# A two-layer decoder on one core: two contexts' values computed earlier and kept in memory, and a new order of the work behind the experts

## The chip, the cores and the metric

The kernel runs on one core of a Trainium2 chip. The time is device microseconds (us) of the whole program on that core; lower is better. TensorE is called PE (its weight loads PEld), VectorE DVE, ScalarE ACT, GpSimd POOL and SyncE SP.

## What is computed

Four sequences (B = 4) of 512 tokens with 256 features pass through six sublayers, each followed by a layer norm: a test-time-training layer, a softmax attention with an additive table (`fside`) over a context of 1601 rows, a mixture of eight experts (two per token), a causal self attention with 16 heads of 16, a 16-head cross attention over the same context with rotated queries and keys, and a feed-forward layer. Everything is float32. The part that the change is about is the cross attention, cut to what matters:

```python
K = (ctx @ Wk.T + bk) -> 16 heads, rotated       # ctx: (4, 1601, 256)
V = (ctx @ Wv.T + bv) -> 16 heads
x = layernorm(x + (softmax(Q K^T / 4 + mask) V) @ Wo.T + bo)
```

The values V need nothing but the context and one 256 x 256 weight (`xaV`; the bias goes into `bob`), so they can be computed at any time.

## The kernel before, in words

**Stages.** The program is one long body, in which each engine's order is mostly written out by hand (`tc.manual_schedule()`); what stands between two such regions is placed by a planner among the neighbours on the same engine. Memory on the core is taken in pools that are closed and opened like a stack, so tiles of a later pool lie where those of a closed one were.

*Test-time training* (ttt, to about 242 us), then *attention with `fside`* (to about 487 us). There `steps` runs over 4 sequences x 4 blocks of 128 tokens: `scored` (L654), `turned` (L684), `weighted` (L706), three blocks deep. The transposed context `ctxT` of a sequence is loaded whole (L639); those of sequences 2 and 3 are in memory when the loop ends. When a sequence's four blocks are done, its `closing` (L719) follows in pieces, one per call of `tail()`: moments and root, the normalization, the transposition `to_xT`, then `route` (L462: the router's matmul on PE, softmax and two choices on DVE, a matmul for the places, then the rows on DVE). For sequences 0 to 2 the next blocks' work fills PE in between; for sequence 3 nothing is left. Behind it stand `scatter(B - 1)` (L772: eight indirect DMAs on POOL that put token rows in `xs`) and `blocks_left` (L773, one small matmul and some 25 small DVE operations), both outside the hand-written order.

*Experts* (L821 on, to about 1024 us): weights for all later stages are loaded first on SP (L824 to L828), then `begin(0)` loads the first rows `xb` from `xs`; 23 blocks of 256 rows follow.

*Behind the experts* (L1588 to L1612): the experts' results are gathered and summed for sequence 0 (`combined(0)`: `fetch`, then `add`, whose last entries are the root and the scaling of the layer norm, then `turn`, the two transpositions), and on PE come the values of contexts 0 and 1 and the keys of context 0 (`keys0`, rotated by DVE at L1149 to L1152), the first self-attention keys and queries (`k0_`, `q0_`) and values (`self_values`, L1134). Each of these takes one of four PSUM banks (`one()`), which ACT empties. Keys go through DRAM (`to_rows`, `from_rows`) to get one head per 32 partitions.

*Attention* (L1638 on): 32 units, 16 of self attention and 16 of cross attention, one for each sequence and group of four heads. A cross unit takes 13 steps of 128 keys. Each step computes scores on PE twice: pass 1 for the next unit (`slot1`, L1229, whose maxima DVE takes at L1267) and pass 2 for this one (`scores`, L1303; exponentials on ACT at L1324), and multiplies the exponentials with the values (`weighted`, L1327). A step has two halves. Other PE work hangs in lists, `extras[i]` for unit i, of which one item goes into a step: with an item, the step's first half carries the whole 512-wide `weighted` and the second half the item; without one, each half carries a 256-wide `weighted` (L1669 to L1684). Among the items are keys (`key`, L1176, rotated on POOL) and values (`value`, L1186: two 256-wide matmuls, each shown as two records, and one ACT copy) of contexts 2 and 3. They are spread by `later` (L1613): 12 key items beside sequence 0's units, 4 key items and 13 values beside sequence 1's, 13 values beside sequence 2's. Their input comes in pieces of 512 columns, two at a time (`chunk`, L1162). The values live in two tiles, `vals[b % 2]`.

Of the kernel before, what the change touches and what calls it, by code (L numbers as in the profile page):

```python
# [9 lines left out]
F32 = mybir.dt.float32  # L10
# [7 lines left out]
P = 128  # L18
B, S, D = 4, 512, 256
S2 = 1601  # L20
NT = S // P
# [13 lines left out]
def kn_of(kt):  # L35
    return P if kt < NKT - 1 else KLAST
# [3 lines left out]
def decoder(ctx: ExitStack, tc: tile.TileContext, a: dict, out: bass.AP):  # L40
# [564 lines left out]
        return wrow, xrow  # L605


    with tc.tile_pool(name="p2", bufs=2) as p2, ExitStack() as ordered:


# [73 lines left out]
        def turned(b, t):  # L684

            sc = scs.pop((b, t))
            pT = p2.tile([P, NKT, P], F32, tag="pT", name="pT")
            for k0 in (0, 8):
                ps = wide()
                flat = ps.rearrange("p a n -> p (a n)")  # L690
                for kt in range(k0, min(k0 + 8, NKT)):
                    kn = kn_of(kt)
                    nc.tensor.transpose(
                        flat[:kn, (kt - k0) * P : (kt - k0 + 1) * P], sc[:, kt * P : kt * P + kn], ident
                    )
# [46 lines left out]
        scored(*steps[0])  # L742
        tails = []

        def tail():
            if tails and next(tails[0], tails) is tails:
                tails.pop(0)

        for i in range(len(steps) + 1):
            if i + 1 < len(steps):  # L750
                b, t = steps[i + 1]
                scored(b, t)
                if t == NT - 1:
                    more_columns(b + 2)
                    if b + 1 < B:
                        queries(b + 1)
            tail()
            if i < len(steps):
                turned(*steps[i])
            tail()  # L760
            if i > 0:
                b, t = steps[i - 1]
                weighted(b, t)
                if t == NT - 1:
                    if b + 1 < B:
                        ctxns[b + 1] = load_ctx(b + 1)
                    tails.append(closing(b))
            tail()
        while tails:
            tail()  # L770
        ordered.close()
        scatter(B - 1, lambda inst: unordered("xs", inst))  # L772
        wrow, xrow = blocks_left()  # L773
    ph2in.close()


# [2 lines left out]


    QS = 1.0 / math.sqrt(HD)
    VW = HD + 1
# [243 lines left out]
    with ExitStack() as s4:  # L1026
# [827 lines left out]
```

## Time and profile before

| | |
|---|---|
| median of three runs | 2437.19 us (2430.2 to 2437.96) |
| the profiled execution, its own time | 2439.88 us |
| its span, first to last instruction | 2438.0 us |
| busy share of the span | PE 96%, DVE 50%, ACT 44%, POOL 17% |

The span by stage, from the trace (the clock is the share of full TensorE speed that was granted):

| us | stage | PE busy | clock |
|---|---|---|---|
| 242 to 487 | attention with `fside` | 240.67 | 0.97 |
| 487 to 523 | `closing(3)`, `blocks_left`, scatter, first `xb` | 10.12 | 0.54 |
| 523 to 1024 | experts | 496.11 | 0.99 |
| 1024 to 1072 | behind the experts | 44.27 | 0.96 |
| 1072 to 1482 | self-attention units | 397.14 | 0.94 |
| 1482 to 1730 | cross units of sequence 0 | 248.00 | 0.98 |
| 1730 to 1976 | of sequence 1 | 246.00 | 1.00 |
| 1976 to 2184 | of sequence 2 | 208.00 | 1.00 |
| 2184 to 2314 | of sequence 3 (no pass 1 for a next unit at its end) | 129.48 | 1.00 |

How to read it: a row of a timeline gives start, duration, engine, line of the kernel, operation, output and inputs, count, and in brackets how long the engine had been idle and what ended that. Matmuls are pipelined, so the durations of neighbours on PE overlap, and the distance between starts says more than the duration. A line such as L202 is that of the helper `mm`, through which most matmuls go; the tile names tell them apart.

### The profile page before, as it was taken

Reading aid. Unit: us, or ns where it says so; the run is one execution under the profiler, and the core shown is the slowest. Engines: PE = TensorE matmul, PEld = TensorE weight load, DVE = VectorE, ACT = ScalarE, POOL = GpSimd, SP = SyncE. Lnnn points to the kernel's source line nnn. Section 1 sums busy time; section 2 is a strip of 40 time slices with the busy share of each in tenths; the row PEclk is TensorE's granted clock in tenths of the full one; section 3 lists DMA queues with packets and bytes.
Section 4 is the critical chain, followed back from the end, with each engine's and each line's share of the span. In section 5 each row is a group of like instructions: output and inputs, shape, how many; then the busy total and the mean of one; then the engine's idle time right before and its main releaser. Section 6 shows DMA issues by size and latency. Waiting matters only on the chain.

```text
span 2438.0 us, 34867 instructions
## 1 busy us (share of the span) xinstructions
PE 2344.4 (96%) x13928; PEld 1328.2 (54%) x13928; DVE 1211.7 (50%) x2854; ACT 1073.5 (44%) x1996; POOL 422.7 (17%) x429
## 2 busy tenths in 40 slices
PE   7898999959999999989999999999999999999998
PEld 4767677748888888843333334333333333333256
DVE  1333334322222233266656667666666666677334
ACT  1111122114444544424555453655666566566730
POOL 1010001121144433345130010222110010000000
PEclk9999999969999999989999997999999999999999
DMA  8300311145667555351211210112110110100100
GB/s 307 150 1 3 124 54 45 49 143 186 247 239 266 198 204 201 124 164 50 66 48 35 95 36 5 39 51 60 51 37 16 45 36 16 30 34 18 31 9 26
DMA packets 76112, 215.84 MB, mean 89 GB/s; under 512 B 11816, under 2 KB 35630, under 8 KB 66862
## 3 DMA queue, kind: packets, MB, share of 16 engines
q1 hardware_dynamic: 61790, 133.04, 16.1%
q0 software_dynamic: 10992, 65.54, 7.3%
q10 hardware_dynamic: 3168, 15.03, 1.8%
q8 instruction: 110, 1.80, 0.3%
q14 instruction: 52, 0.43, 0.1%
HBM read 171.53 MB, written 53.21 MB: 92 GB/s over the span
## 4 chain that ended last, share of the span: by engine, by line
PE 51%; ACT 1%; DVE 1%; issue 0%; DVEq 0%; ACTq 0%
PE s L1310 23%; PE one L202 12%; PE po L1337 11%; PE s L202 2%; PE s L1320 1%; PE one L1295 1%; PE one L1358 1%; ACT x L171 0%; ACT ex L1324 0%; DVE one L1269 0%; PE one L1379 0%; PE one L1477 0%; PE one L1400 0%; DVE pm L1267 0%; DVE st L156 0%
## 5 line engine op out<-in xcount | busy, mean ns | idle before, releaser
L1324 ACT ACTIVATE ex<-s 128x512 f32<-128x512 f32 (+1 forms) x1062 | 577.9, 594 | 466.9 <-PE s L1310 236.7
L1267 DVE TENSOR_REDUCE pm<-one 128x1 f32<-128x512 f32 x768 | 493.7, 685 | 174.5 <-PE s L1310 123.3
L1310 PE MATMUL s<-q,kc 32*128 32x512 f32 x1612 | 524.1, 640 | 0.2 <-ACT ex L1324 0.2
L202 PE MATMUL one<-kc,qt 32*128 32x512 f32 (+1 forms) x2048 | 483.8, 564 | 0.3 <-DVE pm L1267 0.3
L1310 PEld LDWEIGHTS s<-q,kc 32*128 32x128 f32 x1612 | 161.6, 179 | 210.9 <-issue 175.5
L1337 PE MATMUL po<-ex,v 128*32 128x256 f32 (+3 forms) x2472 | 245.1, 465 | 0.3 <-ACT ot L1350 0.3
L1269 DVE CUSTOM_DVE_ANT_0 one<-one,c_diagq 128x512 f32<-128x512 f32 x256 | 171.9, 716 | 75.6 <-PE one L202 63.5
L1310 PE MATMUL s<-q,ks 32*128 32x512 f32 x512 | 179.8, 650 | 5.3 <-ACT ex L1324 4.9
L1337 PEld LDWEIGHTS po<-ex,v 128*32 128x32 f32 (+1 forms) x2472 | 49.8, 108 | 232.2 <-issue 225.5
L886 DVE TENSOR_TENSOR g<-g,sg 128x1024 f32<-128x1024 f32 x46 | 57.2, 1243 | 235.8 <-ACT sg L883 235.7
L202 PE MATMUL wide<-xbT,eWi 128*128 128x256 f32 x736 | 168.9, 389 | 4.0 <-DVE xbT L858 4.0
L202 PEld LDWEIGHTS one<-kc,qt 32*128 32x128 f32 x2048 | 164.2, 188 | 11.6 <-DVE pm L1267 7.9
L202 PE MATMUL wide<-xbT,eWg 128*128 128x256 f32 x736 | 162.6, 379 | 0.0
L202 PE MATMUL bank<-eWo,g 128*128 128x256 f32 x736 | 162.5, 379 | 0.0
L202 PEld LDWEIGHTS wide<-xbT,eWi 128*128 128x128 f32 x736 | 143.5, 196 | 25.8 <-issue 4.2
L202 PE MATMUL one<-ks,qt 32*128 32x512 f32 x512 | 152.6, 665 | 3.7 <-ACT raw L1182 2.7
L202 PEld LDWEIGHTS wide<-xbT,eWg 128*128 128x128 f32 x736 | 139.7, 190 | 19.2 <-ACT g L883 0.2
L1150 POOL TENSOR_TENSOR raw<-raw,c_cos 128x512 f32<-128x512 f32 (+1 forms) x32 | 34.9, 1092 | 660.5 <-DVE swp L1149 578.1
L202 PEld LDWEIGHTS bank<-eWo,g 128*128 128x128 f32 x736 | 138.2, 190 | 17.9
L883 ACT ACTIVATE g<-wide,eWi 128x256 f32<-128x256 f32 x184 | 71.7, 476 | 72.3 <-PE wide L202 69.7
L1310 PEld LDWEIGHTS s<-q,ks 32*128 32x128 f32 x512 | 53.8, 185 | 83.4 <-issue 62.0
L202 PE MATMUL wide<-ctxT,q 128*128 128x512 f32 (+1 forms) x256 | 91.3, 510 | 0.8 <-DVE q L649 0.8
(319 smaller groups left out, 2988.4 us busy)
## 6 DMA issues: line engine op xcount, KB each, us to landing
xs<-zero SPq DMA_DIRECT2D x32, 512.0 KB
kc<-kcd SPq DMA_DIRECT2D x16, 800.5 KB
eWo<-in_eWo SPq DMA_DIRECT2D x8, 1408.0 KB
cx<-in_ctxT SPq DMA_DIRECT2D x18, 512.0 KB
eWi<-in_eWi SPq DMA_DIRECT2D x8, 1028.0 KB
eWg<-in_eWg SPq DMA_DIRECT2D x8, 1028.0 KB
qt<-qd SPq DMA_DIRECT2D x32, 256.0 KB
ctxT<-in_ctxT SPq DMA_DIRECT2D x4, 1601.0 KB
```

The lines of the kernel that those rows point to most:

```text
L202: nc.tensor.matmul(ps, l, r, start=(i == 0), stop=(i == n - 1))
L883: nc.scalar.activation(dst[:, k, :], pv[:, k, :], func, bias=bias)
L886: nc.vector.tensor_tensor(part, part, dst, ALU.mult)
L1150: eng.tensor_tensor(raw[:, :n], raw[:, :n], cos[:, :n], ALU.mult)
L1267: nc.vector.tensor_reduce(pm[:, t, j, c : c + 1], ps, AX.X, ALU.max)
L1269: nc.vector.tensor_tensor_reduce(out=ps, in0=ps, in1=diagq[:, 384 - t * P : 896 - t * P], scale=1.0, scalar=LOWEST, op0=ALU.add, op1=ALU.m ...
L1295: nc.tensor.transpose(pt[:, t * P : (t + 1) * P], ng.rearrange("p j r -> p (j r)"), ident)
L1310: nc.tensor.matmul(ps[:kn], kt[rows, k * P : k * P + kn], q2[rows, :], start=True, stop=cross)
L1320: nc.tensor.matmul(ps[:, k * P : (k + 1) * P], later_[:, :P], later_[:, P:], start=False, stop=True)
L1324: nc.scalar.activation(ex[:kn, h, :], ps[:kn], AF.Exp)
L1337: nc.tensor.matmul(state["po"][j * 32 : j * 32 + 32, q0:q1], (vals if cross else vself)[b % 2][:kn, k, c0 : c0 + 32], ex[:kn, j % 2, q0:q1 ...
L1358: nc.tensor.transpose(pt[:, t * P : (t + 1) * P], ot[:, t * P : (t + 1) * P], ident)
```

## The change

Four things, all in one edit:

1. The 26 values of contexts 2 and 3 (13 blocks of 128 rows each) are computed at the end of the attention with `fside`, from `ctxTs[2]` and `ctxTs[3]`. They stand in three portions in the order of PE and ACT: 3 behind the last `weighted` and the first piece of `closing(3)`, 6 behind the router's matmul and softmax, 17 behind the matmul of `blocks_left`. Two values share a two-bank PSUM tile, a bank each. Their destination is the memory of `fside` (22 blocks) and of half the context rows (4 blocks); `rows_of_values` sets the zeros and ones there on DVE. `blocks_left` moves into the hand-written order, in front of the 17 values, and `scatter(B - 1)` stays behind.
2. Three DMAs on SP write these blocks to two new DRAM tiles `vd` (1.9 MB each): 9 blocks of context 2 behind the ninth value, all 13 of context 3, the last 4 of context 2. The weight `xaV` is loaded once more, early in the stage.
3. In the cross units the 26 values are gone, and with them their eight pieces of context. `later` is now the 8 key items of context 2 beside sequence 0's units and the 8 of context 3 beside sequence 1's. At the start of the second unit of sequences 1 and 2 one DMA on SP reads the next but one values tile from `vd`.
4. Behind the experts `add` stands behind the eighth of context 1's values instead of the thirteenth, `turn` in front of `keys0[4:6]` instead of behind, and `self_values(0)` behind the last keys instead of in front of them.

```diff
+    VW = HD + 1
+    VROW = NH * VW + HD - 1
+    vd = {b: tc.dram_tile((P, NKT * VROW), F32, name=f"vd{b}") for b in (2, 3)}
...
+        xaV = weight(p2, "xaV")
+        values, places, halves = [], {}, []
+
+        def rows_of_values(first):
+            name, tag, n = ("v23", "fs", 22) if first else ("v2", "ctxa", 4)
+            t = p2in.tile([P, NT * S2 if first else KHALF * D], F32, tag=tag, name=name)
...
+            nc.vector.memset(places[3 if first else 2, NKT - 1], 0.0)
+            t = t[:, : n * VROW].rearrange("p (k r) -> p k r", r=VROW)
+            nc.vector.memset(t[:, :, NH * VW :], 0.0)
+            heads = t[:, :, : NH * VW].rearrange("p k (h r) -> p k h r", r=VW)
+            nc.vector.memset(heads[:, :, :, HD : HD + 1], 1.0)
+
+        def value(b, k):
+            kn = kn_of(k)
+            if not halves or len(halves) == 2:
+                halves[:] = [wide()]
+            else:
+                halves.append(halves[0])
+            ps = halves[0][:, len(halves) - 1, :D]
+            mm(ps[:kn], [(ctxTs[b][:, c, k * P : k * P + kn], xaV[:, c, :]) for c in range(2)])
+            dst = places[b, k][:kn, : NH * VW].rearrange("p (h r) -> p h r", r=VW)
+            nc.scalar.copy(dst[:, :, :HD], ps[:kn].rearrange("p (h r) -> p h r", r=HD))
+            if (b, k) == (2, 8):
+                nc.sync.dma_start(vd[2][:, : 9 * VROW], big_of(2, 0, 9))
+            if (b, k) == (3, NKT - 1):
+                nc.sync.dma_start(vd[3], big_of(3, 0, NKT))
+            if (b, k) == (2, NKT - 1):
+                nc.sync.dma_start(vd[2][:, 9 * VROW :], big_of(2, 9, NKT))
...
             if i < len(steps):
                 turned(*steps[i])
+            else:
+                rows_of_values(True)
...
-        while tails:
-            tail()
+        order = [(2, k) for k in range(9)] + [(3, k) for k in range(NKT)]
+        order += [(2, k) for k in range(9, NKT)]
+        values = [lambda b=b, k=k: value(b, k) for b, k in order]
+        for n in (3, 0, 0, 0, 0, 0, 6, 0, 0, 0, 0, 0):
+            if len(values) < len(order):
+                tail()
+            if len(values) == len(order) - 3 and len(places) == 22:
+                rows_of_values(False)
+            for f in values[:n]:
+                f()
+            values = values[n:]
+        assert not tails
+        wrow, xrow = blocks_left()
+        for f in values:
+            f()
         ordered.close()
         scatter(B - 1, lambda inst: unordered("xs", inst))
-        wrow, xrow = blocks_left()
...
-        for f in keys0[0:2] + values1 + add + keys0[4:6] + turn:
+        for f in keys0[0:2] + values1[:8] + add + values1[8:] + turn + keys0[4:6]:
             f()
-        for f in (k0_, q0_, rows0, *self_values(0), *keys0[2:4], *keys0[6:8]):
+        for f in (k0_, q0_, rows0, *keys0[2:4], *keys0[6:8], *self_values(0)):
             f()
...
-        later = [
-            context(2, range(4), ()) + context(3, range(2), ()),
-            context(3, range(2, 4), ()) + context(2, (), range(4)),
-            context(3, (), range(4)),
-        ]
+        later = [context(2, range(4), ()), context(3, range(4), ())]
+        for b in (2, 3):
+            starts[index[b - 1, 1, True]].append(
+                lambda b=b: nc.sync.dma_start(vals[b % 2].rearrange("p k r -> p (k r)"), vd[b])
+            )
```

More of the change, by code (lines that the diff above doesn't have):

```diff
@@ L743, in decoder, with big_of @@
         tails = []
+        xaV = weight(p2, "xaV")
[3 more added lines that the diff above has]
+            t = p2in.tile([P, NT * S2 if first else KHALF * D], F32, tag=tag, name=name)
+            for i in range(n):
+                at = (3, i) if first and i < NKT else (2, i - NKT) if first else (2, 9 + i)
+                places[at] = t[:, i * VROW : (i + 1) * VROW]
+            nc.vector.memset(places[3 if first else 2, NKT - 1], 0.0)
[19 more added lines that the diff above has]
+                nc.sync.dma_start(vd[2][:, 9 * VROW :], big_of(2, 9, NKT))
+        def big_of(b, k0, k1):
+            first = places[b, k0]
+            return bass.AP(first.tensor, first.offset, [first.ap[0], [1, (k1 - k0) * VROW]])
         def tail():
@@ L781, in decoder @@
     QS = 1.0 / math.sqrt(HD)
-    VW = HD + 1
     p4a = late_a.enter_context(tc.tile_pool(name="p4a", bufs=1))
```

## The prediction

> **What bounds the kernel now.** I read the page's busy shares and slices first, then its chain, then the stages, then the timeline at the two places that the change touches.
>
> ```profile
> PE 2344.4 (96%) x13928; PEld 1328.2 (54%) x13928; DVE 1211.7 (50%) x2854; ACT 1073.5 (44%) x1996; POOL 422.7 (17%) x429
> ...
> PE   7898999959999999989999999999999999999998
> ...
> PEclk9999999969999999989999997999999999999999
> ...
> PE 51%; ACT 1%; DVE 1%; issue 0%; DVEq 0%; ACTq 0%
> PE s L1310 23%; PE one L202 12%; PE po L1337 11%; PE s L202 2%; PE s L1320 1%; PE one L1295 1%; PE one L1358 1%; ACT x L171 0%; ACT ex L1324 0%; DVE one L1269 0%; PE one L1379 0%; PE one L1477 0%; PE one L1400 0%; DVE pm L1267 0%; DVE st L156 0%
> ```
>
> PE ends everything that the chain names. One slice, the ninth, is half empty at a low clock: the end of `closing(3)`. In the cross units PE is never free: the list of waits for PE from 1482 to 2314 holds 0.5 us in all. So an item taken from these units shortens the run by its PE time, and one put into the hole costs nothing until the hole is full.
>
> **Part 3, what leaves the cross units.** The groups of lines show the values, and the stage table of this tile that the 104 records of contexts 2 and 3 lie in the units of sequences 1 and 2. The timeline gives one value and the two forms of `weighted`:
>
> ```profile
> 2007.49 1.13 PE L202 MATMUL one<-xaV,cx 128*128 128x256 f32 x4
> ...
> 2060.62 1.06 PE L1337 MATMUL po<-ex,v 128*32 128x512 f32 x8
> ```
> ```profile
> 2064.62 0.64 PE L1337 MATMUL po<-ex,v 128*32 128x256 f32 x8
> ```
>
> By starts: a value holds PE 1.06 us (2007.49 to the scores at 2008.55); the wide `weighted` 0.99 (2060.62 to 2061.61), a half one 0.57 (2064.62 to 2065.19). A step that loses its item goes back to two halves, 1.14 for 0.99. So a value is worth 1.06 - 0.15 = 0.91 us. As a check, the copies of the finished sums (L1350) mark the units' ends: sequence 2's first three take 160.3 us with 10 values and one query item, sequence 3's first three 149.8 with none. Less the query item (2.0 - 0.15), that is 8.7 / 10 = 0.87. I take 0.88: **26 x 0.88 = 22.9 us less**. Ends: the records' whole busy time, 29.3 us; and the worst single pair of units (sequence 2's first 55.3 with 4 values, sequence 3's first 53.6 without), 0.43 each, 11 us. The second would hold if another engine were late next. In a bare half step (1.64 us) ACT is busy 1.08 and DVE 1.29, so both still wait for PE.
>
> Key items only move (12 and 4 become 8 and 8), between units that PE bounds: nothing. Eight pieces of context (SP, 0.46 us an issue) go. The two loads of 1.9 MB stand in SP's queue with key rows, queries and pieces behind them. They overwrite a tile last read by the `weighted` that ended a unit earlier (1706 for a load at 1763), so they don't wait, and DMA is busy 0.10 to 0.15 in these stages. Nothing; if they did hold SP, the rows behind them have a unit's lead.
>
> **Part 1, the hole.** Before, it runs so:
>
> ```profile
> 487.23 0.48 DVE L715 SCALAR_TENSOR_TENSOR r<-bank,rs,x 128x256 f32<-128x256 f32 x1 [4.28 <-PE bank L202]
> ...
> 490.37 2.30 PE L188 MATMUL wide<-ident,x 128*128 128x128 f32 x8 [3.19 <-DVE x L726]
> ...
> 492.71 1.01 ACT L196 COPY xT<-wide 128x1024 f32<-128x1024 f32 x1 [2.84 <-PE wide L188]
> ...
> 505.49 0.64 PE L202 MATMUL bank<-both,before 128*128 128x32 f32 x2 [5.75 <-DVE both L492]
> ```
> ```profile
> 508.35 0.17 DVE L521 SCALAR_TENSOR_TENSOR rows<-eks,ranks 128x8 int32<-128x8 f32 x1 [0.17 <-DVE upto L555]
> ...
> 517.63 0.96 POOL L534 DMA_INDIRECT xs<-x,rows  x1 [0.30 <-issue]
> 520.17 0.89 SPq L835 DMA_DIRECT2D xb<-xs  x2
> ...
> 522.99 1.09 PE L854 MATMUL bank<-ident,xb 128*128 128x128 f32 x4 [15.80 <-DMA xb<-xs]
> ```
>
> The chain is weighted, normalization, router, rows at 508.5, eight scatters at 1.27 us, `xb` issued 520.2, landed 523.0. A value in a row costs 0.89 us at full clock (32 records, 7.14 us at 1024). Portion by portion:
> - 3 values, 2.7 us, fit before the transpositions (487.2 to 490.4). Their copies (0.37 each) stand on ACT behind the root (489.9) and end before the `xT` copy.
> - In two-microsecond windows the clock is 1.00 until 488 and 0.50 from 490 to 530. Now PE works until 489.9, so the transpositions take the 1.04 us that sequence 2's took, and I let the router's matmuls take 3.4 (461.2 to 464.6) for 6.0. The chain gains 1.2 + 2.6 us. [...]
> - 6 values, 5.3 us, lie beside DVE's 5.7 us of choices (499.8 to 505.5); the places' matmul behind them is not held.
> - 17 values are 15.1 us of PE. They begin at 507.2 - 3.8 = 503.4 and end at 518.5, the copy 0.4 later. The scatters now start near 504.8 and have landed near 516.5, so **PE's values take their place as what ends last**: the third store, and with it SP, is free near 519, and `xb` is issued at 519.5 for 520.2.
> - The stores: the zero rows that SP wrote early moved 405 GB/s, so 1.9 MB take 4.7 us. The big one goes out near 515, the last (0.6 MB) at 519; both are through near 522, and `xb` behind them lands near 524.5. That is **1.5 us more** than before. Ends: 1 less (nothing in its way) and 4 more (router cold, stores half as fast).
> - PE is idle some 5 us before `xb`, so the experts' first 32 matmuls stay slow (10.1 us): no gain there.
>
> DVE's new memsets have no row. POOL's of 195 and 208 columns took 0.28 and 0.46, DVE's copy of 512 columns 0.69; three of these are at most 2.1 us in a 4.3 us wait for PE, and three more lie in the 8.5 us behind the normalization: nothing. `blocks_left` no longer interleaves with the rows, which frees 0.2 us of them.
>
> **Part 4, behind the experts.** ACT's root waited for the thirteenth value (row at 1055.24) though DVE was done at 1050.25. Now root and scaling end near 1053.3, but the last five copies stand behind them, and PE has four banks for five values, so it still leaves the values at 1054.9. The transpositions come at 1055.0 instead of 1058.2, but two keys (3.6 us) now stand between them and `k0_`: 1059.6 for 1059.74. Nothing. `self_values` go into the wait for the rows, but need banks that the last two keys hold until ACT reads them (1075.64 and 1077.04, kept by stores of earlier keys). The first scores come near 1077.6 instead of 1072.1; DVE is turning keys until 1078.1 anyway and starts its first maximum near 1079.3 for 1078.2. I take **0.5 us more**; ends -1.5 and +2.
>
> **Sum.** -22.9 + 1.5 + 0.5 = -20.9 us. The profiled execution took 2439.88 (span 2438.0 and 1.9 around it): 2419.0. It stands 2.7 above the median, so 2416 on that scale.
>
> **Rivals**, on the same scale:
> - *The next stage's weight loads go in front of `xb`.* Twelve loads on SP (487.22 to 493.5, 2 MB) lie where the values now lie, and the list of waits shows that the first waited for PE's last `weighted`, the last reader of that memory. Now they wait for the third store, near 522. They stand outside the hand-written order, so the planner may put them before `xb`: 6.2 us of issues, 2 MB in front, `xb` near 531, 8 us late. -22.9 + 8 + 0.5 = -14.4: 2423. For it: they stand first in the text. Against: `xb` is ready a little earlier.
> - *The values were nearly free in the units.* Price 0.43: -11.2 + 2 = -9.2: 2428. For it: that one pair of units; against: all others.
> - *The hole can't take them:* the clock stays at 0.50 there, a value costs 1.7 us (two copies behind the 2.07 us gap at 1048 stand 1.66 apart), 17 take 29, the end is 14 to 18 us later, and the change doesn't do what it says: -22.9 + 18 + 0.5 = -4.4, 2433. Against: PE's gaps are now 0.5 to 1.1 us.
> - *Slower: the stores are slow.* `xb` stands behind them on SP's queue. The key rows (256 KB in rows of 2 KB) took 5.9 us to land, 44 GB/s; at that rate 2.5 MB from 515 on end at 572, and `xb` is 49 us late: +26, 2463. It decides from 23 us late on: 2.5 MB in 30 us, 83 GB/s. Against: the zero rows' 405 GB/s, and 14.9 KB in one piece for each partition.
>
> **Numbers.** Forecast 0.56, weights first 0.22, free values 0.08, hole too small 0.10, slow stores 0.04. A difference of about 0.3% (7.3 us) is the least that a measurement of this kernel can tell from no change: the first three are faster by more, 0.86; the fourth the same, 0.10; the fifth slower, 0.04. The range goes from 2406 (values at 29.3 us, hand-over 1 us shorter) to 2429 (free values); fourth and fifth are left out.
>
> **What would show it.** Right: no L202 on `xaV` from 1482 on; units of sequences 1 and 2 together some 23 us shorter; PE's ninth slice full; the first `xb` matmul within 4 us of 523; the first maximum near 1079. Wrong: the loads of `qkvQ` to `xaO` ahead of `xb`; clock 0.50 during the 17 values; PE waiting for ACT or DVE in bare steps; a wait of SP at the loads from `vd`.

## The result, and the profile after

The changed kernel takes 2431.36 us in the median of 20 runs, the kernel before, on the same chip, 2433.05 us in the median of 20: a ratio of 0.9983, 95% interval 0.997 to 0.9995. That is about 4 us less (1.2 to 7.3; the two medians are 1.7 us apart); 21 us less were forecast. The profiled execution took 2431.25 us, with a span of 2429.5.

The busy shares, the slices and the chain of the changed kernel's page, to be laid beside those of before:

```profile
PE 2343.2 (96%) x14144; PEld 1333.4 (55%) x14144; DVE 1214.0 (50%) x2860; ACT 1075.7 (44%) x1996; POOL 423.6 (17%) x429
...
PE   7898999979999999989999999999999999999998
...
PEclk9999999989999999999999998999999999999999
...
PE 50%; DVE 1%; ACT 1%; issue 0%; DVEq 0%; ACTq 0%
PE s L1368 23%; PE po L1395 12%; PE one L202 11%; PE s L202 2%; PE s L1378 1%; PE one L1353 1%; PE one L1416 1%; ACT x L171 0%; ACT ex L1382 0%; DVE pm L1325 0%; DVE one L1327 0%; PE one L1437 0%; PE one L1535 0%; PE one L1458 0%; DVE nb L166 0%
```

The ninth slice is fuller (7 for 5) and its clock higher (8 for 6): PE does work there now. But PE's busy time is only 1.2 us less, though 26 values moved out of the units: they are the same work in another place, and the gain can only be the time in which PE had been idle. The other weak clock slice, the 25th, lies at the end of the self-attention units, where before has one too (7).

Cut at the same events, the two profiled executions compare like this. "Lost" is the time that PE lost to a half clock, summed over the clock records (length times one minus the granted share); where PE had nothing to do meanwhile, it is more than the clock cost.

| stretch | before (lost) | after (lost) | change | forecast |
|---|---|---|---|---|
| start to the last sum on `r` | 487.23 | 485.00 | -2.2 | 0 |
| the hole: to the first transposition of `xb` | 35.76 (16.6) | 45.98 (4.6) | **+10.2** | +1.5 |
| experts | 501.01 (7.3) | 501.37 (7.3) | +0.4 | 0 |
| hand-over: to the first self-attention maximum | 54.20 (4.1) | 57.01 (3.4) | +2.8 | +0.5 |
| self-attention units | 409.57 (25.6) | 405.22 (20.5) | -4.4 | 0 |
| cross units | 826.09 (1.1) | 810.91 (3.4) | **-15.2** | -22.9 |
| end | 124.15 (3.0) | 123.97 (1.6) | -0.2 | 0 |

The fifth row is clock (409.57 - 25.6 = 384.0, 405.22 - 20.5 = 384.7). The first is not: more was lost to the clock there after (17.1 us) than before (15.4). But this stretch took 482.3 to 487.2 us in the six kernels of this document in which its code is that of before, so its 2.2 us can't be put down to the change. The gain in the units is there, two thirds of its size, and the hole takes two thirds of that back.

The timeline of the changed kernel in the hole (start, duration, engine, line, operation; in brackets the idle time before it and what ended it):

```profile
485.00 0.48 DVE L720 SCALAR_TENSOR_TENSOR r<-bank,rs,x 128x256 f32<-128x256 f32 x1 [3.24 <-PE bank L202]
...
487.55 0.36 ACT L776 COPY v<-wide 128x256 f32<-128x256 f32 x1
...
487.96 1.99 PE L202 MATMUL wide<-xaV,ctxT 128*128 128x256 f32 x8 [2.13 <-ACT v L776]
...
489.79 1.04 PE L188 MATMUL wide<-ident,x 128*128 128x128 f32 x8
...
505.00 0.30 PE L202 MATMUL bank<-both,before 128*128 128x32 f32 x2
...
506.74 0.17 DVE L521 SCALAR_TENSOR_TENSOR rows<-eks,ranks 128x8 int32<-128x8 f32 x1 [0.19 <-DVE eks L516]
...
510.53 1.99 PE L202 MATMUL wide<-xaV,ctxT 128*128 128x256 f32 x8 [0.46 <-ACT v L776]
...
511.70 0.37 ACT L776 COPY v<-wide 128x256 f32<-128x256 f32 x1 [1.22 <-PE wide L202]
...
512.57 0.37 ACT L776 COPY v<-wide 128x256 f32<-128x256 f32 x1 [0.49 <-PE wide L202]
...
512.99 1.99 PE L202 MATMUL wide<-xaV,ctxT 128*128 128x256 f32 x8 [0.46 <-ACT v L776]
...
516.18 0.96 POOL L534 DMA_INDIRECT xs<-x,rows  x1 [0.31 <-issue]
...
526.73 0.32 SPq L782 DMA_DIRECT2D vd<-v  x1
527.14 1.38 SPq L893 DMA_DIRECT2D xb<-xs  x2
...
530.98 1.09 PE L912 MATMUL bank<-ident,xb 128*128 128x128 f32 x4 [4.68 <-DMA xb<-xs]
```

Two things are to be seen. PE is not free to run through the values: eight records (two values) start every 2.46 us, at 510.53 and 512.99, and each time PE has waited 0.46 us for a copy of ACT. And POOL has issued the last scatter by 517.1, but `xb` is issued at 527.1, directly behind the third store, which waited for the last value.

Theory A: two values in one two-bank tile wait for each other. The second value of a pair writes the other bank, but its matmul still waits until ACT has read the first. In the row of 487.96 the second value even waits 2.13 us, since the first one's copy stands on ACT behind the root. Rival: the pace is that of ACT's copies, of the clock or of the matmuls. Theory B, for the units: a bare half step (one without an item) is not bounded by PE alone; rivals are the clock and values that are cheap on PE.

### The profile page after: what moved, and what is told of

It reads as the page before. It is cut to its first block, busy times and chain, and to the rows that moved or that the text cites. A ratio compares the mean times of both kernels' runs of the same rounds, so it can differ in the third digit from the quotient of the medians.

```text
span 2429.5 us, 35297 instructions
## 1 busy us (share of the span) xinstructions
PE 2343.2 (96%) x14144; PEld 1333.4 (55%) x14144; DVE 1214.0 (50%) x2860; ACT 1075.7 (44%) x1996; POOL 423.6 (17%) x429
## 3 DMA queue, kind: packets, MB, share of 16 engines
q1 hardware_dynamic: 60606, 137.66, 16.6%
## 4 chain that ended last, share of the span: by engine, by line
PE 50%; DVE 1%; ACT 1%; issue 0%; DVEq 0%; ACTq 0%
PE s L1368 23%; PE po L1395 12%; PE one L202 11%; PE s L202 2%; PE s L1378 1%; PE one L1353 1%; PE one L1416 1%; ACT x L171 0%; ACT ex L1382 0%; DVE pm L1325 0%; DVE one L1327 0%; PE one L1437 0%; PE one L1535 0%; PE one L1458 0%; DVE nb L166 0%
## 5 line engine op out<-in xcount | busy, mean ns | idle before, releaser
L1368 PE MATMUL s<-q,kc 32*128 32x512 f32 x1612 | 529.5, 640 | 0.8 <-ACT ex L1382 0.8
L1395 PE MATMUL po<-ex,v 128*32 128x256 f32 (+3 forms) x2688 | 252.2, 444 | 0.3 <-ACT ot L1408 0.3
```

Of the source, the lines that this page charges most:

```text
L1368: nc.tensor.matmul(ps[:kn], kt[rows, k * P : k * P + kn], q2[rows, :], start=True, stop=cross)
L1395: nc.tensor.matmul(state["po"][j * 32 : j * 32 + 32, q0:q1], (vals if cross else vself)[b % 2][:kn, k, c0 : c0 + 32], ex[:kn, j % 2, q0:q1 ...
```

## The experiments: the hole

**Own tiles.** Each value takes a new tile and leaves its second bank unused.

```diff
-            if not halves or len(halves) == 2:
-                halves[:] = [wide()]
-            else:
-                halves.append(halves[0])
-            ps = halves[0][:, len(halves) - 1, :D]
+            ps = wide()[:, 0, :D]
```

> The changed kernel, but every value gets a two-bank PSUM tile of its own (one bank used), instead of sharing one with the next value. Measured so far: from the last sum of the attention with the table (DVE's row on r) to the first transposition of xb the kernel before took 35.8 us, the changed one 46.0. Theory A (two values in one tile: the second waits for ACT's copy of the first, so a pair takes 2.46 us): the 17 values then follow each other at 0.89 us, 15.1 instead of 20.7 us, the six earlier ones end about 2 us earlier, and the stretch takes 38 to 40 us; the whole run is 6 to 8 us shorter than the changed kernel, near 2424 where before has 2433. Rival (the pace is set by ACT's copies, by PE's clock or by the matmuls themselves): a pair still takes about 2.4 us and the stretch stays at 45 to 47 us.

Measured: ratio to before 0.9952 (0.9939 to 0.9964), 11.7 us less; the hole is 41.1 us. Its timeline:

```profile
505.89 14.92 PE L202 MATMUL wide<-xaV,ctxT 128*128 128x256 f32 x68
...
521.24 0.32 SPq L778 DMA_DIRECT2D vd<-v  x1
524.09 0.91 SPq L889 DMA_DIRECT2D xb<-xs  x2
...
527.10 1.08 PE L908 MATMUL bank<-ident,xb 128*128 128x128 f32 x4 [6.29 <-DMA xb<-xs]
```

The 17 values (68 records) take 14.9 us in one run without a gap: theory A holds, and the forecast's 15.1 was right for values that don't share a tile. The hole is 1 us longer than expected, though, since `xb` now goes out 2.9 us behind the last store. SP's list of waits names the reason:

```profile
SPq L889 <- DMA xs<-x,rows: 2.5, 1, 2.5
```

The last scatter was issued at 517.75 and the 1.9 MB store at 517.8; from 518 to 524 the DMA engines moved 358 to 424 GB/s (windows of 2 us). Scatters and store collide now.

**Smaller stores, on SP and on ACT's queue.** Both build on own tiles.

```diff
-            if (b, k) == (2, 8):
-                nc.sync.dma_start(vd[2][:, : 9 * VROW], big_of(2, 0, 9))
...
+            for c, k0, k1 in ((2, 0, 3), (2, 3, 9), (3, 0, 4), (3, 4, 8), (3, 8, NKT), (2, 9, NKT)):
+                if (b, k) == (c, k1 - 1):
+                    nc.sync.dma_start(vd[c][:, k0 * VROW : k1 * VROW], big_of(c, k0, k1))
```

> Values in tiles of their own, as in e1_own_tiles (17 values in 14.9 us, but xb issued at 524.1, 2.9 us behind the third store, since the last scatters landed late; hole 41.1 us), and the values go out in six stores instead of three (3, 6, 4, 4, 5, 4 blocks), each when its last block is copied. Theory C (the 1.9 MB store issued at 517.8 fills the DMA engines just when the last scatters and xb want them): the last big piece is 0.7 MB, the scatters land near 519 to 520, xb goes out right behind the last store at 521.3 to 521.7, hole 38 to 39 us. Rival (the scatters are late for another reason, such as POOL's order): xb stays 2.5 to 3 us behind the last store, hole near 41.

> As e5_six_stores, but the stores are issued from ACT's queue instead of SP's, so that xb on SP doesn't stand behind them. Theory C with SP's order as the next limit: xb is issued when the scatters have landed, near 519.5 to 520.5, hole 37 to 38 us. Rival 1 (the values on PE or the weight loads hold xb): as e5, 38 to 39. Rival 2 (issuing on ACT delays the copies and so PE): values at over 0.95 us each, hole over 40.

Measured: six stores on SP 0.9932 (0.9916 to 0.9949), hole 40.0 us; on ACT's queue 0.9918 (0.9888 to 0.9948), hole 40.2. Both missed their 37 to 39. The collision is gone (in the first, `xb` goes out at 521.9 even before the last store), but from the ninth or tenth of the 17 values on ACT's copies come late, several of them 1.41 to 1.46 us apart, and SP's list says that `xb` waits for PE's last matmul on `wide` (1.6 and 2.5 us). So `xb` is tied to the values in a way that I had not counted, and no queue helps it. Presumably its memory is that of something these matmuls read; which tile that is was not followed up.

**One value beside ACT's copy of `xT`.** First alone on the changed kernel, then together with own tiles, stores on ACT's queue and the old order behind the experts:

```diff
-        for n in (3, 0, 0, 0, 0, 0, 6, 0, 0, 0, 0, 0):
+        for n in (3, 0, 0, 0, 1, 0, 5, 0, 0, 0, 0, 0):
```

> The changed kernel with one number list changed: the portions are 3, 1, 5, 17 instead of 3, 6, 17, so that one value lies between the transpositions and the router's matmuls. Pairs of values still share a tile, the stores stay on SP. Theory D (that one value keeps PE's clock at 1.00 through the router's matmuls): rows, 21.7 us behind the last sum in the changed kernel, come 18 to 19 us behind it; the 17 values still take 20.7 us, so xb moves by the same 3 us: hole 42.5 to 43.5 us for 46.0. Rival (only the freed stores and tiles of e7_one_beside_copy made the difference there): hole 45 to 46.

> As e6_stores_on_act, with the old order behind the experts, and the portions 3, 1, 5, 17 instead of 3, 6, 17: one value lies between the transpositions and the router's matmuls, beside ACT's copy of xT. If PE's clock falls at 492 because the window before holds too little work, the added value keeps it up, the router's matmuls take 3.4 to 4 us instead of 5.6, the places' matmul comes 2 to 4 us earlier, and the hole shrinks to 34 to 36 us, less than before. Rival (the clock falls during the router's short matmuls whatever stands before them): the router and the 5 values still run at 0.50, and only one value's time is won, hole 36 to 38. Old order: first values to first maximum 50 to 54 us instead of 56 to 57.

Measured: alone 0.9955 (0.9938 to 0.9971), hole 45.5, so the rival was nearer: three of the four router blocks run at full clock in the changed kernel too, and pairs of values still wait. (The ratio is lower than the changed kernel's 0.9983, with intervals that touch, but the two profiled executions are only 0.6 us apart, so nothing is read from that.) Together 0.9926 (0.9909 to 0.9942), hole 36.8, just longer than the 34 to 36 expected. There the step works for the router, though the clock falls behind it. Two windows of the kernel with own tiles, then three of the one with the added value (columns: length, then busy time of PE, PEld, DVE, ACT and POOL, the granted clock, DMA share, GB/s):

```profile
488.90:492.30 3.40, 1.98 (x11) 1.28 (x12) 1.66 (x7) 1.55 (x3) 0.97 (x1) 1.00 0.13 46
492.30:495.70 3.40, 3.40 (x16) 3.28 (x15) 0.00 (x0) 0.00 (x0) 0.96 (x1) 0.51 0.11 39
```
```profile
489.30:492.70 3.40, 2.51 (x12) 1.59 (x12) 1.90 (x7) 1.94 (x6) 1.67 (x2) 1.00 0.46 173
492.70:496.10 3.40, 3.38 (x24) 3.23 (x24) 0.00 (x0) 0.25 (x1) 0.97 (x2) 1.00 0.11 39
496.10:499.50 3.40, 3.40 (x10) 2.75 (x10) 2.58 (x13) 0.60 (x2) 0.96 (x1) 0.50 0.19 67
```

With the value, the stretch in which the router's 24 matmuls lie has the full clock, 3.4 us for 5.6, and the rows stand 17.8 us behind the last sum instead of 21.1. All seven kernels with own tiles agree: 3.4 us for the router in the four with the value, 5.6 to 5.9 in the three without. In the last row but one PE is busy for 3.38 of 3.40 us with the router's eight-column matmuls, and the clock still falls behind them, in the last row. So a busy share of 3.38 of 3.40 us did not keep the clock up here. What kept it up through the router, in the kernels with own tiles, was one value of 256 columns: without it PE was busy for 1.98 of the 3.40 us up to 492.3, and the clock fell there; with it PE was busy for 2.51 of the 3.40 us up to 492.7, and the clock stayed. More of what the clock goes by these runs don't show (in the changed kernel PE was busy for 2.47 of the 3.40 us up to 494.4, and the clock fell there). The half-clock stretches in the clock records are 3.4 us long or multiples of it: the one that begins in the hole of the kernel before, at 489.8, is 41.0 us long; the two that begin in the hole of the changed kernel, at 494.4 and 528.5, are 6.8 and 10.2 us long.

**Where do the slow last values come from?** With six stores ACT's copies stand still from the ninth or tenth of the 17 values on, whichever queue issues the stores. The next two kernels have five and three stores.

```diff
-            for c, k0, k1 in (..., (3, 0, 4), (3, 4, 8), (3, 8, NKT), (2, 9, NKT)):
+            for c, k0, k1 in (..., (3, 0, 4), (3, 4, NKT), (2, 9, NKT)):
```

> As e7_one_beside_copy (own tiles, portions 3, 1, 5, 17, old order behind the experts, stores on ACT's queue), but context 3's last two stores are one (five stores in all). There the last values but four followed each other at 1.43 us instead of 0.86, since ACT's copies stood 1.06 us apart without a reason in the profile, from the store of context 3's second piece on; e5_six_stores showed the same on SP's queue, e1_own_tiles with one store for context 3 did not. If that store is what slows the copies, the 17 values take 15 us again, and the hole is 34 us instead of 36.8, below the 35.8 of before; the run then is 19 to 21 us shorter than before. Rival (something else at this place): 36.5 to 37.

> Own tiles, portions 3, 1, 5, 17, old order behind the experts, and the three stores on SP as in the changed kernel (9, 13 and 4 blocks). It differs from e7_one_beside_copy by the stores alone. There ACT's copies stood up to 2.5 us apart near the end of the 17 values, for no reason that the profile shows, with six and with five stores; in e1_own_tiles with three they did not. If more stores bring these gaps: the 17 values take 15 us, the last ends near 517.5, but the 1.9 MB store goes out near 514 beside the last scatters, and xb waits for these as in e1_own_tiles: hole 37 to 39 us, run 17 to 19 us shorter than before. If the gaps have another cause they stay, and the hole is 39 to 41 us.

Measured: five stores 0.9938 (0.9923 to 0.9954), hole 37.6; three stores on SP 0.9948 (0.9931 to 0.9966), hole 40.7. The gaps stay with five stores and with three, so their number is not what brings them. The timeline of the kernel with three:

```profile
511.62 0.37 ACT L772 COPY v<-wide 128x256 f32<-128x256 f32 x1 [0.65 <-PE wide L202]
...
514.48 0.37 ACT L772 COPY v<-wide 128x256 f32<-128x256 f32 x1 [2.48 <-PE wide L202]
...
514.90 1.13 PE L202 MATMUL wide<-xaV,ctxT 128*128 128x256 f32 x4 [0.89 <-issue]
```

The 17 values started at 504.27; at 0.86 us each, as up to there, the second of these copies (the ninth of the 17) was due near 512.4. PE, which may be three tiles ahead, then waits for it. So the last nine copies went to DVE, which has nothing left to do there:

```diff
-            nc.scalar.copy(dst[:, :, :HD], ps[:kn].rearrange("p (h r) -> p h r", r=HD))
+            copy = nc.vector.tensor_copy if (b, k) in order[17:] else nc.scalar.copy
+            copy(dst[:, :, :HD], ps[:kn].rearrange("p (h r) -> p h r", r=HD))
```

> As e7_one_beside_copy (hole 36.8 us there), with the copies of the last nine values on DVE, which is through with the rows by then, instead of ACT. If ACT itself stands still there (its copies wait only for PE, which had long been done), DVE's copies follow PE at 0.86 us each, the 17 values take 15 us, xb goes out 2 to 3 us earlier and the hole is 34 to 35 us; the run is 19 to 21 us shorter than before. Rival (PE or the PSUM banks hold the values up there, whoever copies): 1.43 us each again, hole 36.5 to 37.5.

Measured: 2413.23 us for 2432.5, ratio 0.9925 (0.9912 to 0.9938), about 18 us less, a little under the 19 to 21 expected. It is shorter than the changed kernel, whose interval (0.997 to 0.9995) lies above it. From the same kernel with ACT's copies (0.9926) and the one with six stores on ACT's queue (0.9918) the whole time can't tell it; what the copies on DVE do is read from the timeline.

```profile
506.23 0.42 DVE L773 COPY v<-wide 128x256 f32<-128x256 f32 x1 [0.74 <-PE wide L202]
...
507.09 0.42 DVE L773 COPY v<-wide 128x256 f32<-128x256 f32 x1 [0.44 <-PE wide L202]
...
513.13 0.42 DVE L773 COPY v<-wide 65x256 f32<-65x256 f32 x1 [0.44 <-PE wide L202]
513.88 0.93 SPq L887 DMA_DIRECT2D xb<-xs  x2
```

DVE's copies follow each other every 0.86 us to the end: it was ACT that stood still, not PE or PSUM. Why it did remains open. The hole is 36.3 us, not the 34 to 35 expected: `xb` now lands 4.4 us after its issue (2.8 before). The last store, issued at 513.6, moved from 514 to 517, and nearly all of `xb`'s data after that. So 26 values stand in a hole that is 0.5 us longer than the empty one (35.7 to 36.2 us in the six kernels that have it empty).

## The experiments: the cross units

**Only the units.** The values are left out of the kernel before, once with the keys as in the change, once with the keys where they were.

```diff
-            context(2, range(4), ()) + context(3, range(2), ()),
-            context(3, range(2, 4), ()) + context(2, (), range(4)),
-            context(3, (), range(4)),
+        later = [context(2, range(4), ()), context(3, range(4), ())]
```

> The kernel before with the 26 values of contexts 2 and 3 left out altogether (the units of sequences 2 and 3 use the values that lie in the two tiles from contexts 0 and 1), and the keys of contexts 2 and 3 spread as in the changed kernel. Nothing else differs, no work is added anywhere, so its time is the price of these values in the cross units. The prediction's 0.88 us for a value: 22.9 us shorter than before, about 2410 where before has 2433. Theory B (a step that loses its value takes 3.49 us, not 3.28, because every second half step waits for a score bank that ACT still reads; a value is worth 0.77): 20 us shorter. The stretch in which the values now stand stays at 35.8 us in both. Rival (values nearly free, 0.43): 11 us shorter.

> As e3_units_only (values of contexts 2 and 3 left out of the kernel before, nothing put in their place), but the keys of contexts 2 and 3 stay where they were: 12 key items beside sequence 0's units, 4 beside sequence 1's. Prediction's step: moving four key items costs nothing, so the cross units take the same 808 to 811 us as in e3_units_only (807.6 there without its clock dip of 6.8 us at half clock). Units of sequence 1 then show 13 values by themselves. Rival (a key item costs more where values were, or less): a difference of over 1 us between the two sums at equal clock.

Measured: 0.9934 (0.9922 to 0.9946), 16.1 us less, and 0.9928 (0.9903 to 0.9952). In the first the cross units take 811.0 us with 3.4 lost, exactly as in the changed kernel, so nothing of the shortfall there comes from the loads of `vd` or from anything else that the change added. At equal clock that is 826.09 - 1.1 - 807.6 = **17.4 us** for values and keys, between the 20 of theory B and the 11 of its rival. The second splits it: 13 values of sequence 1's units are worth 215.75 - 209.63 = 6.1 us, 0.47 each, 13 of sequence 2's 213.71 - 204.16 = 9.6 us, 0.73 each; and moving four keys, forecast at nothing, saves 6.7 us beside sequence 0 and costs 5.2 beside sequence 1, 1.5 us less. Neither group of values is worth 0.88 each. Why, a stretch of bare steps in the changed kernel shows (PE and ACT):

```profile
2042.20 0.69 PE L1368 MATMUL s<-q,kc 32*128 32x512 f32 x1
...
2042.22 1.10 PE L1368 MATMUL s<-q,kc 32*128 32x512 f32 x2
...
2043.27 0.64 PE L1395 MATMUL po<-ex,v 128*32 128x256 f32 x8
...
2043.41 1.08 ACT L1382 ACTIVATE ex<-s 128x512 f32<-128x512 f32 x2 [0.89 <-PE s L1368]
2043.84 0.69 PE L1368 MATMUL s<-q,kc 32*128 32x512 f32 x1
...
2044.06 0.89 PE L1368 MATMUL s<-q,kc 32*128 32x512 f32 x2
...
2045.11 0.64 PE L1395 MATMUL po<-ex,v 128*32 128x256 f32 x8
...
2045.68 0.69 PE L1368 MATMUL s<-q,kc 32*128 32x512 f32 x1
```

The half step from 2042.20 takes 1.64 us, the next one 1.84. In the first the second score matmul starts 0.02 us after the first, in the second 0.22 later: there are three banks for scores, a half step takes two, and the second of them is still being read by ACT's first exponential (2043.41 + 0.54 = 2043.95). All of the delay lies in front of that second score matmul: from it to `weighted` it is 1.05 us in both half steps, and from there to the next half step 0.57, so `weighted` does not wait for its exponentials. The list of waits for PE hardly shows any of this, since PE is filled with the other matmuls meanwhile. The list for its weight loads does, in the kernel before (us in total, times, longest):

```profile
PEld s L1310 <- ACT ex L1324: 33.9, 73, 1.0
```

Two bare steps take 6.97 us here (2042.20 to 2049.17); where the kernel before has a step with a value and a bare one in turn, the two take 7.69 (2051.80 to 2059.49). The value is worth the difference, 0.72 us, as in sequence 2's units.

**Four score banks.**

```diff
-        ps2 = s4.enter_context(tc.tile_pool(name="ps2", bufs=3, space=PSUM))
-        ps1 = s4.enter_context(tc.tile_pool(name="ps1", bufs=4, space=PSUM))
+        ps2 = s4.enter_context(tc.tile_pool(name="ps2", bufs=4, space=PSUM))
+        ps1 = s4.enter_context(tc.tile_pool(name="ps1", bufs=3, space=PSUM))
...
-                reduces = [next1() for _ in range(min(2, ends1[u] + LEAD - done["n"]))]
+                reduces = [next1()]
```

> The changed kernel, with four PSUM banks for the second pass's scores instead of three, and three instead of four for the first pass's and all items (and the first-pass pieces that run ahead of a unit go one at a time). Theory B (in a bare step every second half waits 0.2 us for a score bank that ACT still reads, 1.85 instead of 1.64 us): bare halves are 1.64 us each as far as the first pass's banks allow; the cross units of sequence 3, which have few items, show it, 48.8 us for the third of them before. If DVE's maxima then hold the three other banks in the same way, the halves keep 1.75 us on the mean or get longer. Rival (the longer halves have nothing to do with score banks): 1.64 and 1.85 alternate as before and the waits for ACT stay.

Measured: 2% slower, 1.0204 (1.0187 to 1.0221), cross units 849.5 us. The timeline in bare steps (PE and DVE):

```profile
2107.16 0.69 PE L1368 MATMUL s<-q,kc 32*128 32x512 f32 x1
...
2108.36 1.29 DVE L1325 TENSOR_REDUCE pm<-one 128x1 f32<-128x512 f32 x2 [0.98 <-PE s L1368]
...
2108.80 0.69 PE L1368 MATMUL s<-q,kc 32*128 32x512 f32 x1
...
2109.11 0.81 PE L1368 MATMUL s<-q,kc 32*128 32x512 f32 x2
...
2110.73 0.69 PE L1368 MATMUL s<-q,kc 32*128 32x512 f32 x1
```

1.64 and 1.93: the wait has moved to the first pass's banks and grown. The second score matmul starts 0.31 us after the first, behind a first-pass matmul whose bank is free when the first of DVE's two maxima ends (2108.36 + 0.65 = 2109.01). Banks are the limit, but this run doesn't say that ACT is what holds the score banks. The next two do.

**ACT's part cut short.** Fixed tiles for the exponentials, zeroed once, and:

```diff
             for h, ps in enumerate(pair):
-                nc.scalar.activation(ex[:kn, h, :], ps[:kn], AF.Exp)
+                n = 256 if u[2] else S
+            nc.scalar.activation(ex[:kn, h, :n], ps[:kn, :n], AF.Exp)
```

> The kernel before, with the exponentials of the cross units cut to 256 of their 512 columns (the other half of each tile keeps zeros or older numbers, so the cross attention is not the reference's), and the tiles for them fixed and zeroed once. It takes away what theory B names: ACT then frees a score bank some 0.2 us earlier. Theory B: bare half steps are 1.64 us each instead of 1.64 and 1.85, so the third unit of sequence 3 (48.75 us before, ten steps or more without an item) takes 46 to 47 us, and the cross units together some 10 us less than before's 826. Rival (the longer halves have nothing to do with ACT): 48.7 and 826 as before.

> As e12_short_exponents, and the 26 values left out and the keys spread as in the changed kernel (as in e3_units_only). The difference of the cross units between the two, at equal clock, is the price of the values where ACT does not hold the score banks. With ACT as it is that price was 826.1 - 1.1 - 807.6 = 17.4 us. Theory B: 22 to 24 us here, the prediction's 26 x 0.88 = 22.9, so the prediction's price was PE's time for a value and the shortfall is the wait for score banks. Rival (a value is simply cheaper on PE than its records say): 17 to 18 us here too.

Both kernels leave out more than these two texts say. The line that computes the exponentials stands behind the loop, so of the two in a half step the first is left out altogether, and only the second is computed, in the cross units with 256 of its columns. There are 531 exponentials instead of 1062, and the self-attention units have half of theirs too (374.1 us instead of 384.0 at equal clock). The exponential left out is the one that reads the bank which the next half step's second score matmul needs, so what theory B names is taken away whole, and not only shortened by 0.2 us.

Measured: 0.9815 (0.9795 to 0.9835) and 0.9729 (0.9709 to 0.975). The cross units take 800.1 us (1.2 lost) with the values and 777.5 (1.3 lost) without: the 26 values and the keys' move are worth **22.6 us** here, where the prediction had 22.9 and the kernel as it is 17.4. The third unit of sequence 3 is 46.2 us for 48.75. The timeline without the values (PE and ACT):

```profile
2030.72 0.69 PE L1313 MATMUL s<-q,kc 32*128 32x512 f32 x1
...
2032.07 0.38 ACT L1329 ACTIVATE ex<-s 128x256 f32<-128x256 f32 x1 [1.26 <-PE s L1313]
...
2032.37 0.69 PE L1313 MATMUL s<-q,kc 32*128 32x512 f32 x1
...
2034.01 0.69 PE L1313 MATMUL s<-q,kc 32*128 32x512 f32 x1
...
2035.64 0.69 PE L1313 MATMUL s<-q,kc 32*128 32x512 f32 x1
```

Every half step is 1.64 us, and the weight loads' wait for ACT's exponentials goes from 33.9 us to 5.7 in the first of the two. Theory B holds: where ACT's exponentials don't hold the score banks, a value that leaves is worth what PE spends on it. That 22.6 comes so close to 22.9 is partly luck: the 13 values of sequence 2's units are worth 12.7 us here, 0.98 each, for 0.73 with all exponentials, and the rest is 13 values together with the keys' move, which this pair does not split. (With the values still in, the cross units are 26 us shorter than before, where some 10 were expected of shortened exponentials. That part of the computation is left out, so it is no gain.)

## The experiments: behind the experts

The old order on the changed kernel, and the new order alone on the kernel before (the two loops at the end of the diff).

> The changed kernel with the old order behind the experts (add behind all thirteen values, turn behind keys0[4:6], self_values in front of the last keys). Stretch from the first of context 0's values behind the experts to the first self-attention maximum: 54.2 us before, 57.0 in the changed kernel. Theory (the new order delays the first scores, since they stand behind self_values, whose banks wait for ACT): 54 to 55 us here, the run 2 to 3 us shorter than the changed kernel. Rival (what the order costs here comes back in the self-attention units, 409.6 us before and 405.2 after): the stretch is shorter by 3 us and the units longer by 3 to 4, the run the same within 1 us.

> The kernel before with nothing but the new order behind the experts. Prediction's step: 0.5 us more (ends 1.5 less, 2 more). Theory from the trace of the changed kernel: the stretch from the first values to the first self-attention maximum goes from 54.2 to 57 us; if that is not given back in the units, the run is 2 to 3 us longer. Rival: given back, the run the same within 1 us.

Measured: the old order on the changed kernel 0.9975 (0.9964 to 0.9985), against 0.9983 with the new one, intervals that overlap; the new order alone 1.0002 (0.9989 to 1.0014). By stretches, less the time lost to the clock: hand-over 49.5 us with the old order and 53.6 with the new one in the changed kernel, 50.1 and 51.5 in the kernel before; the units 384.0 to 384.7 in all four. So the new order costs 1.4 to 4.1 us there in these two pairs, and at equal clock nothing comes back. One execution of each says little, though: over all kernels of this document the hand-over, less the lost time, is 47.8 to 52.6 us with the old order (ten kernels, mean 50.3) and 51.5 to 53.6 with the new one (seven, mean 52.4), so about 2 us. In the whole time that is too little to tell. The changed kernel shows how:

```profile
1084.07 0.32 ACT L1240 ACTIVATE raw<-one,bk 128x65 f32<-128x65 f32 x1 [6.87 <-DMA kcd<-raw]
...
1084.43 3.78 PE L202 MATMUL one<-qkvV,xT 128*128 128x256 f32 x8 [6.05 <-ACT raw L1240]
...
1089.37 0.70 DVE L1327 CUSTOM_DVE_ANT_0 one<-one,c_diagq 128x512 f32<-128x512 f32 x1 [2.48 <-PE one L202]
```

ACT waits 6.87 us for a store of an earlier key to free its tile (4.54 in the kernel before), the values of self attention behind it wait for the bank, and the first scores stand behind these.

## Why the prediction was wrong

Three stretches missed: the hole by 8.7 us (10.2 for 1.5), the units by 7.7 (15.2 for 22.9), the hand-over by 2.3 (2.8 for 0.5). (The lower end of the range, 2406, leaves out the 1.5 us of the hole; nothing rests on that.)

- **Part 1, "17 values are 15.1 us of PE": the step that failed.** They took 20.7 us, 5.6 of the 8.7. The diff says that two values share a tile, and I took the pace of single tiles (0.89 us) from another stage; a wait of one bank's writer for the other bank's reader was not in the sum. With own tiles it is 14.9 us.
- **"the router's matmuls take 3.4" and "6 values, 5.3 us ... is not held": failed too,** and with them the 17 values began 20.6 us behind the last sum where I had 16.2, another 4.4 us. The clock fell at 494.4, the router took 4.1 us and the six values 8.8, and the places' matmul came at 505.0 though its input was ready at 502.4. The rows came 21.7 us behind the last sum (21.1 before), where I had them some 17 behind it. One value of 256 columns beside the `xT` copy, with own tiles, kept the clock up through the router (3.4 us).
- **That PE's values end last, and that SP's third store then holds `xb`: right,** and the reason why each late microsecond of the values was a late microsecond of `xb`. Beside it stand two ties that I had not named: `xb` waits for the values' last matmul, and stores and scatters collide. `xb` landed in 3.8 us for my 5, the term of the hole that was better than forecast.
- **Part 3, "In a bare half step ... both still wait for PE": wrong by a fifth of a microsecond every second half step,** and worth 22.9 - 17.4 = 5.5 us in all; the values alone gave 15.7, which is 7.2 short. The trace of before had it: its half steps at 2048.38, 2050.01 and 2051.80 are 1.63 and 1.79 us apart. I took the shorter one for all, and of the lists of waits I took PE's (0.5 us) and not that of its weight loads (33.9 us for ACT's exponentials). "PE waiting for ACT or DVE in bare steps" was my own sign of being wrong, and it came. My check by units (0.87) compared units of different sequences and hid it. "Key items only move ... nothing" was 1.5 us in the forecast's favour. Another 2.3 us were a half clock of 6.8 us at 2177 where before had lost 1.1; the same dip stands in six of the other kernels without values there, half of it in two and none in five, and half of it in one with the values, so I can't put it down to the change.
- **Part 4: the mechanism as described** (scores behind `self_values`, whose banks wait for ACT), about 2 us on the mean for 0.5 (1.4 and 4.1 in the two pairs; my ends were -1.5 and +2): the last two keys' tiles came free only at 1084.1, behind a wait of 6.87 us for an earlier key's store.
- **The rivals.** Weight loads ahead of `xb` did not come (they are issued from 530.2 on), slow stores neither (330 to 390 GB/s). "The hole can't take them" came true in its size (4.4 us less forecast), which is luck, by a cause that it did not name: not a half clock, but two banks of one tile. "Values nearly free" was wrong in size (0.47 to 0.73 for 0.43) and right in the reason that I had let go: another engine is late next.

## What to carry to other kernels

Before work goes into an idle stretch, look at what each piece waits for there: in this program two results in one PSUM tile wait for each other's reader even though they lie in different banks (17 values took 20.7 us, in tiles of their own 14.9), and a pace taken from another stage holds only with the same tiles. The price of an item that leaves a full engine is the difference of the whole steps with and without it, read from start to start over a full period, because the next limit (here a bank that ACT still reads) may lie only 0.2 us behind; and a list of an engine's waits can hide such a limit that the list of its weight loads shows (0.5 us against 33.9). An idle stretch on a chain can be filled nearly for free (26 values for 0.5 us of hole); here that took own tiles, a clock kept up through the chain's small steps (the router's matmuls in 3.4 us for 5.6), and stores that don't stand in the chain's queue.

## What the runs showed of the hardware

- The half-clock stretches of PE are 3.4 us or multiples of it, 3.4 to 41.0 us in the kernel before and 3.4 to 20.5 in the changed one (but for the one that the end of the run cuts off). In one kernel, eight-column matmuls that kept PE busy for 3.38 of 3.40 us were followed by one; the 3.4 us before, with PE busy for 2.51 us, 256-column matmuls among it, were not.
- ACT's copies of 256 columns stood still for 1.03 to 2.5 us, several times from the ninth or tenth of 17 values on, in five kernels while their input was ready; DVE's copies in the same place did not. The cause is open.
- Stores of 4.6 to 14.9 KB for each partition moved 310 to 424 GB/s in windows of 2 us. Beside one of 1.9 MB the last scatters landed so late that SP waited 2.5 us for them.
